# Graph kernel: dealing the steps of the next pair's preparation out between the groups of slots of each gather

## The chip, the cores and the metric

The kernel runs on one core of a Trainium2 chip. The time is device microseconds of one launch. Before the change the median of three runs was 3244.12 us (3240.37 to 3251.95). One further execution was recorded by the hardware profiler; its own time was 3232.01 us. In what follows PE is the tensor engine, DVE the vector engine, ACT the scalar engine, POOL the GpSimd engine, and SP the engine that only issues transfers. Each takes its own queue of instructions.

## The reference

There are 16 graphs of 1024 nodes with 64 channels, each with its own 1024x1024 adjacency matrix. Two layers, each with a residual, are computed:

```
h = relu(layernorm(x))                       # layer 0
neigh = (adj > 0) & not self;  nb = neighbours of a node;  rank = position of a neighbour in its row
skip = ceil(nb / 2) if nb > 10 else 1
drop neighbour j of i if skip > 1 and rank % skip == skip - 1      (and symmetrically j, i)
s = sort of the live neighbours' h, itself included, for each channel
agg = .25 * quantile(s, .25) + .5 * quantile(s, .5) + .25 * quantile(s, .75)   # interpolated
x = x + (relu((h + agg) W1 + b1) W2 + b2)
h = relu(layernorm(x))                       # layer 1
x1, x2, x3 = three steps of bn(relu(adj (x W) + b)), each from the one before
x = x + relu(concat(x1, x2, x3) Wl + bl)
```

The costly part is the sort: for each of 16 x 1024 nodes and 64 channels, some 11 to 42 values are put far enough in order to read three quantiles.

## The kernel before

**Pairs.** Two graphs are handled together, one in each half of the 128 partitions (64 channels each), so there are 8 pairs. Nodes are renumbered by their number of live neighbours, so that columns with like counts stand together. They are cut into seven blocks of columns plus a tail of 16 columns (`BLOCKS`, `TAIL`); a block of 200 columns has 11 slots for neighbours, the last 48 columns have 26, and the tail 42. The tails of four pairs (then of the other four) are sorted together in the fifth and in the last pair (`TAILS`).

**Preparation of a pair.** `prepare` is a generator, which yields after each of 81 small steps. For each of the two graphs `prepare_one` loads the adjacency matrix in eight tiles `a`, converts them (`edge` L662 on ACT, `junk_v` L664 on DVE) and transposes them on PE (`ptE` L669, evicted to `edgeT` L672), counts the neighbours (`tot` L643, `sums` L648, `nbp` L683, `nb` L687), numbers and drops neighbours (`cs` L708 and L713, `stays` L717 and L718, `q` L728 to L739, `edge` L744), makes a key per node (`key` L750, `keys` L755) and from it the node's place in the order (`place` L765 on DVE). POOL then scatters the rows to their places in DRAM with eight indirect transfers (L770). `find_live` loads them back in eight tiles `lp` (L786, from POOL's queue, with two buffers), transposes them on PE (`pt` L796) and counts again (`nv_all` L808); `number_slots` writes to `r` (L838) the number of the slot that a neighbour takes. `half` and `z` (L611, L614) are what the quantiles need; `z` is the first thing that a pair's first gather and sort have, and is taken below as the pair's start.

**Gather and sort of a block.** `gather` goes through a block's slots in groups. For a group, DVE compares `r` with the slot's number and writes a 0/1 matrix `s` (L962, two buffers), PE multiplies the features `hp` with it into `pg` (L993, three PSUM buffers), and ACT copies `pg` to `g` (L998). `sort_block` runs a network of minima and maxima over the slots on DVE (L920), weights them (L925, L933; coefficients on ACT, L855 and L858) and sends the sums to DRAM (`store`, with a transposition `pt_agg` L1005).

**Second half of the net.** `later` is also a generator. For a pair it loads what is needed and gathers agg back into the order of the nodes with 16 indirect transfers on POOL (L1172), adds h (L1071), and runs the small multiplications of layer 0 and the three steps of layer 1 (`pw` L1113, `pg` L1129, `py` L1084).

**Order.** In the main loop, while pair p is gathered and sorted block by block, the preparation of pair p+1 goes on: ahead of the gather of each next block stand 11 steps of it. At the eighth turn the rest is run, and the next pair's first block is gathered. In the last pair there is nothing left to prepare, and 7 steps (`STEPS`) of `later` take their place:

```
for p in range(NP - 1):
    ahead = Steps(prepare(p + 1, early))
    for n in range(last + 1):
        for _ in range(11):
            ahead.step()
```

The order in which the program is written is a priority only. A scheduler, with costs of its own for each instruction, decides from the priorities and the dependencies the order in which each engine's queue holds its instructions; on the chip that order is fixed.

Of the kernel before, what the change touches and what calls it, by code (L numbers as in the profile page):

```python
# [29 lines left out]
STEPS = 7  # L30
# [329 lines left out]
def missing_high(slots, least):  # L360

    return range(slots - 1, least, -2)
# [37 lines left out]
def graph_layers_kernel(ctx: ExitStack, tc: tile.TileContext, ins, out: bass.AP):  # L400
    nc = tc.nc
    x_d, adj_d, mask_d = ins["x"], ins["adj"], ins["nodemask"]
    NB, N, _ = x_d.shape
# [96 lines left out]
    def column(name, rows, twice=False):  # L500
        t = const.tile([rows * (1 + twice), 1], F32, name=f"c_{name}")
        for k in range(1 + twice):
            nc.scalar.dma_start(out=t[k * rows : (k + 1) * rows, :], in_=ins[name].rearrange("(p o) -> p o", o=1))
        return t
# [19 lines left out]
    for i in (1, 2, 3):  # L524
        wl = const.tile([P, P], F32, name=f"wl{i}")
        both(wl, ins[f"L1_gnn_W{i}"])
        bl, g, be, m, v = (column(f"L1_gnn_{k}{i}", C, True) for k in ("b", "g", "be", "m", "v"))
# [16 lines left out]
    def bias(value):  # L544

        if value not in biases:
            t = const.tile([P, 1], F32, name=f"bias{len(biases)}")
            nc.vector.memset(t, value)
            biases[value] = t
        return biases[value]  # L550
# [382 lines left out]
            nc.vector.tensor_tensor(o, a, b, ALU.add)  # L933
            i -= k

    def gather(st, block, g, pools):


        work, ps, _ = pools
        j0, j1, least, slots = block  # L940
        first, end, fewer = NEAR[(BLOCKS + (TAIL,)).index(block)]
        W = j1 - j0
        high = missing_high(slots, least)
        r, at = (st.r[0], j0) if j1 <= SPLIT else (st.r[1], j0 - SPLIT)
        per = max(1, min(HALF // W, 400 // W))
        for k0 in range(0, slots, per):
            n = min(per, slots - k0)

            w0 = fewer.get(k0, 0)
            if w0 == W:  # L950
                w0 = 0
            chunks = [
                range(
                    max([c for c in first if k0 + k >= first[c]], default=0),
                    min([c for c in end if k0 + k < end[c]], default=NT),
                )
                for k in range(n)
            ]
            s = work.tile([P, n, 2, NT, W], BF16, tag="s", bufs=2, name="s")
            for k, us in enumerate(chunks):  # L960
                us = slice(us.start, us.stop)
                nc.vector.tensor_scalar(  # L962
                    s[:, k, :, us, w0:], r[:, :, us, at + w0 : at + W], float(LIVE + 1 + k0 + k), None, ALU.is_equal
                )
            pg = ps.tile([P, n, W], F32, tag="pg", bufs=3, name="pg")
            looks = [(u, [k for k in range(n) if u in chunks[k]]) for u in range(NT)]
            looks = sorted((look for look in looks if look[1]), key=lambda look: -len(look[1]))
            whole = len(looks[0][1]) == n and not w0
            if not whole:
                for x in range(2):  # L970

                    nc.tensor.matmul(
                        out=pg[x * C : (x + 1) * C].rearrange("p k w -> p (k w)"), lhsT=ident_h[C:, :C],
                        rhs=st.hp[C:].rearrange("p a x t c -> p (a x t c)")[:, : n * W], start=True, stop=False,
                    )
            for i, (u, ks) in enumerate(looks):
                if i == whole:
                    for k in range(n):
                        if k0 + k + 1 not in high:
                            continue  # L980
                        none = work.tile([P, W], BF16, tag="none", bufs=2, name="none")
                        nc.scalar.activation(
                            none, st.nvs[:, j0:j1], AF.Relu, bias=bias(k0 + k + 0.5), scale=-1.0
                        )
                        for x in range(2):
                            half = slice(x * C, (x + 1) * C)
                            nc.tensor.matmul(
                                out=pg[half, k], lhsT=ident_big[:, half], rhs=none, start=False, stop=False
                            )
                ks = slice(ks[0], ks[-1] + 1)  # L990
                for part in range(3):
                    for x in range(2):
                        nc.tensor.matmul(  # L993
                            out=pg[x * C : (x + 1) * C, ks, w0:], lhsT=st.hp[:, part, x, u, :],
                            rhs=s[:, ks, x, u, w0:], start=(whole and i == 0 and part == 0),
                            stop=(i == len(looks) - 1 and part == 2),
                        )
            nc.scalar.copy(g[:, k0 : k0 + n, :], pg)  # L998
# [9 lines left out]
        for x in range(2):  # L1008
            nc.scalar.dma_start(out=agg_d[2 * p + x][place0 : place0 + n, :], in_=o[:n, x * C : (x + 1) * C])

    def gather_block(st, n, pools):
        work, ps, rows = pools
        block = (BLOCKS + (TAIL,))[n]
        j0, j1, _, slots = block
        if n == 0:
            for q in range(len(TAUS)):
                nc.gpsimd.tensor_copy(tail_z[:, q, st.p, :], st.z[:, q, TAIL[0] : TAIL[1]])
        st.g[n] = rows.tile([P, slots, j1 - j0], F32, tag="g", bufs=2, name="g")
        gather(st, block, st.g[n], pools)

    def sort_block(st, n, pools):

# [326 lines left out]
    with ExitStack() as stack:  # L1349
        keep = stack.enter_context(tc.tile_pool(name="keep", bufs=1))  # L1350
        pools = (
            stack.enter_context(tc.tile_pool(name="work", bufs=1)),
            stack.enter_context(tc.tile_pool(name="ps", bufs=1, space=PSUM)),
            stack.enter_context(tc.tile_pool(name="rows", bufs=1)),
        )
        last = len(BLOCKS)
        with ExitStack() as inner:
            early = (
                inner.enter_context(tc.tile_pool(name="early", bufs=1)), keep,
                inner.enter_context(tc.tile_pool(name="ps_early", bufs=1, space=PSUM)),  # L1360
            )

            ahead = Steps(prepare(0, early))
            ahead.rest()
            st = ahead.result
            gather_block(st, 0, pools)
            for p in range(NP - 1):
                ahead = Steps(prepare(p + 1, early))
                for n in range(last + 1):
                    for _ in range(11):  # L1370
                        ahead.step()
                    if n == 0 and p in TAILS:

                        sort_block(st, n, pools)
                        gather_block(st, n + 1, pools)
                        sort_tails(*TAILS[p], pools)
                        continue
                    if n < last:
                        gather_block(st, n + 1, pools)
                    else:  # L1380
                        ahead.rest()
                        gather_block(ahead.result, 0, pools)
                    sort_block(st, n, pools)
                st = ahead.result


        with ExitStack() as inner:
            one = inner.enter_context(tc.tile_pool(name="late", bufs=1))
            late = (one, inner.enter_context(tc.tile_pool(name="ps_late", bufs=2, space=PSUM)))
            done = Pair()  # L1390
            done.sent = TAILS[NP - 1][0]
            ahead = Steps(later(late, done))
            for n in range(last + 1):
                for _ in range(STEPS):
                    ahead.step()
                if n == 0:
                    sort_block(st, n, pools)
                    gather_block(st, n + 1, pools)
                    sort_tails(*TAILS[NP - 1], pools)
                    done.sent = NP - 1  # L1400
                    continue
                if n < last:
                    gather_block(st, n + 1, pools)
                sort_block(st, n, pools)
            done.sent = NP
            ahead.rest()
# [46 lines left out]
```

## Time and profile before

| What | Value |
|---|---|
| median of three runs | 3244.12 us |
| profiled execution, its own time | 3232.01 us |
| its span, first to last instruction | 3230.2 us |
| granted clock of the tensor engine | 0.902 |
| DVE, PE, ACT, POOL busy | 2569.1, 2602.9, 1714.2, 461.8 us |
| preparation of the first pair | 0 to 196 us |
| start of the eight pairs (`z`, L614) | 196, 496, 803, 1110, 1421, 1800, 2113, 2418 us |
| last pair with `later` beside it | 2418 to about 2913 us |
| rest of `later` | about 2913 to 3230 us |

A pair thus takes 300 to 314 us, the one in which tails are sorted 379 us. Busy shares are means over stages with different limits, so single stretches are looked at. In a line of the waits, the left side is the instruction that waited, the right side what came last before it could start, and then follow total us, number of times and the longest. In a timeline, the time in brackets is how long the engine had been idle, and what ended that.

### The profile page before, as it was taken

Reading aid. Unit: us, or ns where it says so; the run is one execution under the profiler, and the core shown is the slowest. Engines: PE = TensorE matmul, PEld = TensorE weight load, DVE = VectorE, ACT = ScalarE, POOL = GpSimd, SP = SyncE. Lnnn points to the kernel's source line nnn. Section 1 sums busy time; section 2 is a strip of 40 time slices with the busy share of each in tenths; the row PEclk is TensorE's granted clock in tenths of the full one; section 3 lists DMA queues with packets and bytes.
Section 4 is the critical chain, followed back from the end, with each engine's and each line's share of the span. In section 5 each row is a group of like instructions: output and inputs, shape, how many; then the busy total and the mean of one; then the engine's idle time right before and its main releaser. Section 6 shows DMA issues by size and latency. Waiting matters only on the chain. (4 is left out here: it accounts for less than half of the span.)

```text
span 3230.2 us, 67236 instructions
## 1 busy us (share of the span) xinstructions
PE 2602.9 (81%) x27819; PEld 1728.7 (54%) x27849; DVE 2569.1 (80%) x5895; ACT 1714.2 (53%) x3292; POOL 461.8 (14%) x545
## 2 busy tenths in 40 slices
PE   3689968987898689867686799689976689898878
PEld 2446645664566357545463466456644356565545
DVE  4149999899889988998997889988996888793332
ACT  4777647655766566666464666476553223242221
POOL 4111020110011001200112010201112120221110
PEclk9779989998999799988797799889988799899999
DMA  4131113011311130114001211130102110222211
GB/s 136 46 105 66 37 44 123 33 35 32 118 33 37 42 107 33 51 54 97 31 17 45 91 48 34 45 117 32 39 21 61 21 42 17 54 55 53 53 53 41
DMA packets 221082, 177.45 MB, mean 55 GB/s; under 512 B 189024, under 2 KB 189152, under 8 KB 216672
## 3 DMA queue, kind: packets, MB, share of 16 engines
q1 hardware_dynamic: 141824, 125.88, 12.7%
q0 software_dynamic: 17408, 37.81, 3.8%
q10 hardware_dynamic: 61536, 9.39, 1.9%
q8 instruction: 219, 3.59, 0.5%
q14 instruction: 95, 0.78, 0.1%
HBM read 124.44 MB, written 48.55 MB: 54 GB/s over the span
## 5 line engine op out<-in xcount | busy, mean ns | idle before, releaser
L993 PE MATMUL pg<-s,hp 128*64 128x400 bf16 (+11 forms) x16848 | 1361.8, 314 | 93.2 <-DVE s L962 92.7
L993 PEld LDWEIGHTS <-hp 128*64 128x64 bf16 x16848 | 907.4, 113 | 452.1 <-issue 75.3
L962 DVE TENSOR_SCALAR s<-r 128x3200 bf16<-128x3200 bf16 (+25 forms) x1312 | 621.1, 520 | 144.2 <-PE pg L993 143.9
L998 ACT COPY g<-pg 128x400 f32<-128x400 f32 (+10 forms) x384 | 168.5, 442 | 478.2 <-PE pg L993 440.4
L920 DVE TENSOR_TENSOR t<-g 128x600 f32<-128x600 f32 (+9 forms) x524 | 319.8, 628 | 12.9 <-ACT g L998 11.1
L770 POOL DMA_INDIRECT live_d<-edge,place x128 | 175.4, 1371 | 1025.3 <-DVE place L765 870.9
L1129 PE MATMUL pg<-adjT,xw 128*64 128x512 fp8e4 x2304 | 285.5, 400 | 39.6 <-DVE xw L1119 28.9
L920 DVE TENSOR_TENSOR g<-t 128x96 f32<-128x96 f32 (+16 forms) x555 | 285.8, 539 | 1.4
L855 ACT ACTIVATE coef<-z,bias 128x200 f32<-128x200 f32 (+6 forms) x480 | 174.8, 402 | 140.9 <-DVE agg L933 133.7
L1129 PEld LDWEIGHTS <-xw 128*64 128x64 bf16 x2304 | 144.7, 115 | 163.1 <-DVE xw L1119 30.3
L1172 POOL DMA_INDIRECT agg<-agg_d,place x128 | 139.4, 1089 | 535.7 <-PE pt L1060 412.8
L920 DVE TENSOR_TENSOR t<-t 128x192 f32<-128x192 f32 (+20 forms) x447 | 208.5, 478 | 0.4
L796 PE MATMUL pt<-ident_h,lp 128*128 128x128 bf16 x1024 | 102.3, 261 | 120.8 <-DMA lp<-live_d 71.1
L786 POOL DMA_DIRECT2D lp<-live_d x128 | 87.5, 685 | 774.0 <-PE pt L796 745.4
L664 DVE SCALAR_TENSOR_TENSOR junk_v<-a 128x1024 fp8e4<-128x1024 f32 x128 | 156.3, 1221 | 49.2 <-DMA a<-in_adj 49.0
L858 ACT ACTIVATE coef<-coef,wcol 128x200 f32<-128x200 f32 (+7 forms) x512 | 190.7, 399 | 3.5 <-issue 2.2
L799 ACT ACTIVATE liveT<-pt 128x1024 fp8e4<-128x1024 f32 x128 | 129.9, 1024 | 98.7 <-PE pt L796 97.6
L838 ACT CAST r<-pr 128x592 bf16<-128x592 f32 (+1 forms) x256 | 143.5, 587 | 48.6 <-PE pr L834 47.4
L832 PE MATMUL pr<-liveT,upto 128*128 128x512 fp8e4 (+2 forms) x384 | 124.7, 343 | 50.3 <-ACT r L838 41.3
L796 PEld LDWEIGHTS <-lp 128*128 128x128 fp8e4 x1024 | 82.9, 117 | 145.0 <-DMA lp<-live_d 101.0
L762 ACT ACTIVATE junk<-keys,minus 128x1024 fp8e4<-128x1024 f32 x128 | 144.4, 1128 | 29.8 <-PE keys L755 28.7
L744 ACT ACTIVATE edge<-q,bias 128x1024 fp8e4<-128x1024 f32 x128 | 142.0, 1110 | 33.1 <-PE q L739 29.1
(182 smaller groups left out, 3956.6 us busy)
## 6 DMA issues: line engine op xcount, KB each, us to landing
a<-in_adj SPq DMA_DIRECT2D x128, 512.0 KB, 3.4
adjT_d<-edgeT SPq DMA_DIRECT2D x16, 1024.0 KB, 4.4
lp<-live_d POOLq DMA_DIRECT2D x128, 128.0 KB, 2.3
adjT<-adjT_d SPq DMA_DIRECT2D x16, 1024.0 KB, 6.3
room<-in_x SPq DMA_DIRECT2D x16, 256.0 KB, 3.2
h_d<-room SPq DMA_DIRECT2D x16, 256.0 KB, 2.9
h_again<-h_d SPq DMA_DIRECT2D x16, 256.0 KB, 3.8
xt<-in_x SPq DMA_DIRECT2D x16, 256.0 KB, 4.7
```

What stands on the lines that cost most here:

```text
L664: nc.vector.scalar_tensor_tensor(junk, a, 1.0, a, ALU.is_equal, ALU.not_equal, accum_out=odd[:, b, t : t + 1], saturate=False)
L762: nc.scalar.activation(junk, keys, AF.Sign, bias=minus[:, t : t + 1], accum_out=above[:, t : t + 1], saturate=False)
L770: sent = nc.gpsimd.indirect_dma_start(out=live_d[b][:, :], out_offset=bass.IndirectOffsetOnAxis(ap=place[:, b, t : t + 1], axis=0), in_=ed ...
L796: nc.tensor.matmul(out=pt[:, u, :], lhsT=lp[:, u * P : (u + 1) * P], rhs=ident_h, start=True, stop=True)
L838: nc.scalar.copy(st.r[side][:, x, u, :], pr[:, : j1 - j0])
L855: nc.scalar.activation(coef[:, i, :], z[:, at], AF.Abs, bias=bias(rank - (slots + 1) // 2 + tau), scale=sign)
L858: nc.scalar.activation(coef[:, i, :], coef[:, i, :], AF.Relu, bias=wcol[:, q : q + 1], scale=-w)
L920: nc.vector.tensor_tensor(view(bufs, o, n1, n2), view(bufs, a, n1, n2), view(bufs, b, n1, n2), ALU.max if op else ALU.min)
L962: nc.vector.tensor_scalar(s[:, k, :, us, w0:], r[:, :, us, at + w0 : at + W], float(LIVE + 1 + k0 + k), None, ALU.is_equal)
L993: nc.tensor.matmul(out=pg[x * C : (x + 1) * C, ks, w0:], lhsT=st.hp[:, part, x, u, :], rhs=s[:, ks, x, u, w0:], start=(whole and i == 0 an ...
L998: nc.scalar.copy(g[:, k0 : k0 + n, :], pg)
L1129: nc.tensor.matmul(out=pg[cs, :], lhsT=part[:, u, cs], rhs=adjT[x][:, u, sl], start=(u == 0 and k == 0), stop=(u == NT - 1 and k == len(xw ...
```

## The change

`gather` takes a generator of steps and a number, and runs that many steps spread evenly over the groups of slots: ahead of each group as many as are due by the slots that are then done. The 11 (in the last pair 7) steps ahead of each gather fall away. So a gather whose block has, say, five groups has one to three steps ahead of each group. The number of steps for each block is the same, and the steps themselves are the same; ahead of the next pair's first gather the rest of the preparation is still run whole, now without the 11 steps before it (four steps are then left, the same as before). In the two turns with tails, and in the first turn of the last pair, the sort of the first block now stands ahead of the steps. In the last turn of the last pair the 7 steps stay as they were.

```diff
-    def gather(st, block, g, pools):
+    def gather(st, block, g, pools, between):
...
         for k0 in range(0, slots, per):
             n = min(per, slots - k0)
+            if between is not None:
+                steps, count = between
+                for _ in range(count * (k0 + n) // slots - count * k0 // slots):
+                    steps.step()
...
-        gather(st, block, st.g[n], pools)
+        gather(st, block, st.g[n], pools, between)
...
             for p in range(NP - 1):
                 ahead = Steps(prepare(p + 1, early))
                 for n in range(last + 1):
-                    for _ in range(11):
-                        ahead.step()
                     if n == 0 and p in TAILS:
 
                         sort_block(st, n, pools)
-                        gather_block(st, n + 1, pools)
+                        gather_block(st, n + 1, pools, (ahead, 11))
                         sort_tails(*TAILS[p], pools)
                         continue
                     if n < last:
-                        gather_block(st, n + 1, pools)
+                        gather_block(st, n + 1, pools, (ahead, 11))
                     else:
                         ahead.rest()
                         gather_block(ahead.result, 0, pools)
...
             for n in range(last + 1):
-                for _ in range(STEPS):
-                    ahead.step()
                 if n == 0:
                     sort_block(st, n, pools)
-                    gather_block(st, n + 1, pools)
+                    gather_block(st, n + 1, pools, (ahead, STEPS))
                     sort_tails(*TAILS[NP - 1], pools)
                     done.sent = NP - 1
                     continue
                 if n < last:
-                    gather_block(st, n + 1, pools)
+                    gather_block(st, n + 1, pools, (ahead, STEPS))
+                else:
+                    for _ in range(STEPS):
+                        ahead.step()
                 sort_block(st, n, pools)
```

More of the change, by code (lines that the diff above doesn't have):

```diff
@@ L1009, in store, with gather_block @@
             nc.scalar.dma_start(out=agg_d[2 * p + x][place0 : place0 + n, :], in_=o[:n, x * C : (x + 1) * C])
-    def gather_block(st, n, pools):
+    def gather_block(st, n, pools, between=None):
         work, ps, rows = pools
```

## The prediction

> **What bounds the kernel now.** I read the busy times first, then the stretches, then the waits of one stretch, then single events.
>
> ```profile
> PE 2602.9 (81%) x27819; PEld 1728.7 (54%) x27849; DVE 2569.1 (80%) x5895; ACT 1714.2 (53%) x3292; POOL 461.8 (14%) x545
> ```
>
> Two engines are equally full, so the bound changes by place. The stretch from 520 to 840 us, a pair and the start of the next, has PE busy 271.3 and DVE 292.2 of 320 us: inside the pairs DVE leads. From 2900 us on DVE is busy 117.1 of 330 and PE 269.8: the tail after the last sort is PE's. The chain of the page covers 3% of the span, so I did not use it. Waits of DVE and PE in 520 to 840 us (engine, waiting line, what came last: total us, times, longest):
>
> ```profile
> DVE s L962 <- PE pg L993: 14.5, 10, 3.0
> DVE junk_v L664 <- DMA a<-in_adj: 6.6, 8, 1.9
> ...
> PE pt_agg L1005 <- DVE agg L933: 13.2, 4, 10.3
> PE pt L796 <- DMA lp<-live_d: 7.5, 3, 5.4
> ...
> PE pg L993 <- DVE s L962: 6.2, 4, 3.9
> PE q L728 <- ACT edge L744: 2.4, 1, 2.4
> ```
>
> DVE loses some 27 us per pair, half of it because the two buffers of `s` are still being read by matmuls. Only work that closes these holes can make a pair shorter; its 292 us of DVE work stay.
>
> The last view is the timeline of the fourth period (z of L614 at 803 us): start, duration, operation, and idle time before it. On POOL, scatters and loads of live rows share one queue:
>
> ```profile
> 1014.92 1.10 POOL L770 DMA_INDIRECT live_d<-edge,place  x1 [7.48 <-DVE place L765]
> ...
> 1025.54 2.40 POOL L770 DMA_INDIRECT live_d<-edge,place  x1 [0.31 <-ACT liveT L799]
> 1027.94 1.40 POOL L786 DMA_DIRECT2D lp<-live_d  x2
> ```
>
> On PE and on DVE, what came after:
>
> ```profile
> 1030.41 0.40 PE L796 MATMUL pt<-ident_h,lp 128*128 128x128 bf16 x2 [5.48 <-DMA lp<-live_d]
> ...
> 1038.97 1.86 DVE L962 TENSOR_SCALAR s<-r 128x1152 bf16<-128x1152 bf16 x5 [2.74 <-PE pg L993]
> ```
>
> The reader should see one chain. The second graph's place (L765, 211.7 us into the pair) releases eight scatters, 13 us of POOL. Behind them stand the sixth to eighth load of the first graph. PE waits 5.5 us for the sixth, gather groups queue behind that, and DVE waits 2.7 us for their buffer.
>
> **What the Trainium skill says.** "Perfetto Trace Analysis", section "Tensor Engine Instruction", calls ACT, DVE and GPSIMD strict FIFO and gives PE only a limited reorder. The lines above agree: nothing passes the blocked tile. "DMA: Bandwidth & Descriptors", section "Anatomy of one DMA", puts about 2 us of fixed cost on a GpSimd DMA; loads of live rows here land in 2.3 us. "SBUF — State Buffer", section "A bandwidth-pool intuition that's wrong", says that some VectorE operations lock GpSimd out of writing descriptors. The trace may show it once: most scatters take 1.0 to 1.5 us, but in the pair with tails, at 1689.0 us, one took 14.4 us.
>
> **The change part by part.** I compared the order of each engine's instructions in the two built programs and gave every instruction its duration of before. Positions below are so much work into a pair's queue. No instruction is added in the seven pairs, POOL's order is unchanged, and SP's loads of `a` move by a place or two against the adjT_d store. PE's and DVE's sequences are the same at the start of a pair (to 39 and 54 us of work) and at its end (DVE from 286 us on). So only holes between can change.
>
> *First graph.* Groups 9 and 12 of `s` come earlier on DVE (58.1 to 54.1, 83.6 to 73.3); key and place of the first graph later (111.9 to 132.2, 126.9 to 137.8). Before, PE waited 3.9 us for `s` at 47.7 us into the pair, 2.3 for agg at 90.3, and smaller pieces for edgeT and nbp; behind these it ran 12.3 us behind its own work through the second gather. In the new order I find a lag of 9.6. DVE follows PE there: its waits from 124.6 to 136.1 us are 0.7, 1.9, 2.5 and 2.8, together 7.9. It gains the 2.7 and some of the next groups' slack, taken as 3.5. Against it, nb (L687) of the second graph now reaches DVE ahead of its sums and nbp on PE: about 1.8. Net -1.7, at most -6 if all of the 7.9 falls but that 1.8. PE's 2.4 us wait for edge (L744) also goes, but PE then waits for lp anyway: nothing.
>
> *Second graph.* Its place moves on DVE from 216.1 to 231.5 us of work; on the old clock that is from 211.7 to 225.1 us, +13.4. Each step keeps its own price: 0.5 to the first scatter, 13 for eight, 2.5 for the load, hence 241.1 us. PE comes to the sixth tile 4.9 us of work later (208.8 to 213.7) with a lag larger by 1.1: at 227.9 instead of 221.9. It stands for 13.2 us, where it stood 5.5. The group cut in two by this tile feeds `s` of group 41, which stands 3.7 us earlier on DVE (249.3 to 245.6). DVE has some 4.6 us to spare, so it waits 8.6 instead of 2.7: +5.9, and about +1 for the next groups, which follow PE. Tiles 13 to 16 are now spread among gather groups (+3.4 to +7.9), so the 2.4 us wait at 273.4 us goes: -2.4. Later slips of PE fall into its 10.3 us wait for agg at 292.8, the cover at the end: were it gone, they would cost up to 5. Net +4.5.
>
> A pair: -1.7 + 4.5 = +2.8; I take +2, because part of the +1 behind the tile may find slack too. Bounds are -4 (all first-graph holes close, the tile costs only +2) and +9 (nothing gained, lateness reaches DVE whole). Seven pairs: +14. In the pair with tails the 21.3 us that DVE lost at 307.9 us belong to the long scatter. I take it as recurring; without it that pair is 17 us shorter.
>
> *Last stage.* Its sums (L1071) wait for indirect gathers:
>
> ```profile
> DVE agg L1071 <- DMA agg<-agg_d,place: 50.1, 5, 15.2
> DVE s L962 <- PE pg L993: 18.4, 8, 4.5
> ```
>
> Sixteen gathers take POOL some 20 us and 2.4 to land. The DVE work between the first issue and L1071 is, before to after, 10.6 to 61.7 us for the second pair (its wait was 15.2: gone), 20.4 to 21.9 for the third (10.4, -1.3), 17.9 to 16.3 for the fourth (11.9, +1.4), and 42.5 to 30.3 for the fifth (1.6, +10.6 if the queue is as late). Sum -4.5. PE has 8.5 us less done when the tails are sorted, part of which returns in the PE-bound rest, estimated at 1.5. Net -3, bounds -15 and +12. The some 318 us after 2913 us are the same instructions: 0.
>
> *Sum.* The profiled execution took 3232.0 us (span 3230.2). 3232.0 + 14 - 3 = 3243. The median shown is 3244.12, 12.1 above it; with that, 3255.
>
> **The rivals.**
>
> *Clearly slower.* A longer lateness per pair. For it: the scatter that took 14.4 us shows that this queue can lose more than its 13 us, and place now falls among the dense small operations of the fifth and sixth sort. Against: the other pairs' scatters show no such loss. With +9 a pair: 3232 + 63 - 3 + 12 = 3304.
>
> *Faster.* The other side, by one mechanism: DVE's waits on `pg` in the first half are holes that the old clumps of preparation make on PE. Dealt out, PE keeps ahead. With -4 in seven pairs: 3232 - 28 - 3 + 12 = 3213. It decides where PE's stand at the sixth tile stays under some 10 us: DVE then waits under 5.8, which with +1 and -2.4 costs less than the 1.7 gained. For it: the 14.5 us of waits. Against: the position of place, which is a fact of the queue.
>
> *No change.* The program's order is only a priority, both ends of a pair are in the same order, and gains and losses cancel: 3244. For it: only 25 us of holes exist in a normal pair. That the deal hardly alters the queues is excluded by the positions above.
>
> **How the numbers follow.** A difference of 0.3%, about 10 us, is what a measurement of this kernel can tell from none. Forecast 0.38, own range 3246 to 3275; its low end, 0.05, counts as the same. Clearly slower 0.22, no change 0.18, faster 0.22. So faster 0.22, same 0.05 + 0.18 = 0.23, slower 0.33 + 0.22 = 0.55. The range leaves out a tenth on each side: 3222 to 3305, between the rivals' ends.
>
> **What would show it.** Right: in a normal pair the DVE wait for `pg` near 235 us into it grows from 2.7 to about 8 us, PE's wait for lp from 5.5 to about 13, place of the second graph falls some 10 us later, and the group of waits at 124 to 136 us shrinks by 3 us. In the last stage the 15.2 us wait at L1071 is gone and the fifth grows. Pair periods of 300 to 311 us become some 2 us longer. Wrong: if periods fall, the lp wait was absorbed; if they rise by 8 or more, look at the scatters' durations and at what POOL waits for. It would also fail if the tails or the L1071 waits change by more than 15 us.

## The result

| | before | after |
|---|---|---|
| median | 3244.4 us (4 runs, 3240.4 to 3252.0) | 3289.6 us (4 runs, 3280.5 to 3293.5) |
| profiled execution, span | 3230.2 us | 3278.5 us |
| ratio | | 1.0133 (95% interval 1.0110 to 1.0157) |

The change costs some 45 us. The time lies inside the predicted range (3222 to 3305), on the predicted side, but above the forecast's own range (3246 to 3275) and four times as far from no change as the forecast had it, nearer to the rival that was called clearly slower (3304). Both profiled executions had a mean granted clock of 0.902.

The busy times of the page of the changed kernel:

```profile
PE 2620.0 (80%) x27826; PEld 1725.6 (53%) x27849; DVE 2568.8 (78%) x5895; ACT 1709.4 (52%) x3292; POOL 474.0 (14%) x545
```

DVE has the work it had (2569.1 us before), and its share fell: the 48 us by which the span grew are holes, stretches in which DVE waits. Where they are, the distances between the pairs' starts (L614) tell:

| stage | before, us | after, us | difference |
|---|---|---|---|
| six pairs without tails, sum | 1842.5 | 1897.5 | +55.0 (+14.2 in the first pair, +3.8 in the sixth) |
| pair with tails | 379.2 | 372.3 | -6.9 |
| last stage, to the last sum of the sort | 495.1 | 490.6 | -4.5 |
| preparation of the first pair, and the rest of `later` after the sort | | | +4.6 |

A pair without tails loses 9.2 us on average. Lines of the `gather` stand four lower in the changed kernel (L962 is L966, L993 is L997, L998 is L1002). Take the period that the prediction reads (called the fourth there, the first being the preparation ahead of the first pair): before it ran from 802.7 to 1110.2 us, now from 828.5 to 1146.5. Waits of DVE:

```profile
DVE s L966 <- PE pg L997: 24.4, 6, 11.3
DVE t L920 <- ACT g L1002: 3.5, 2, 2.8
...
DVE key L750 <- ACT edge L744: 3.0, 1, 3.0
```

and of PE:

```profile
PE pt L796 <- DMA lp<-live_d: 11.7, 2, 9.8
PE pt_agg L1009 <- DVE agg L933: 9.4, 3, 8.1
...
PE pg L997 <- DVE s L966: 5.9, 2, 4.3
PE keys L755 <- DVE key L750: 5.2, 2, 2.8
```

In the same period before, `s` waited in ten shorter pieces, DVE had no wait for key, and PE's wait for it was 0.5 us:

```profile
DVE s L962 <- PE pg L993: 16.0, 10, 2.8
```

Now there are fewer waits and longer ones. They are in two places.

**The second graph.** The timeline of POOL (start, duration, operation, idle time before):

```profile
1055.80 4.32 POOL L770 DMA_INDIRECT live_d<-edge,place  x1 [2.51 <-DVE s L966]
...
1069.47 0.96 POOL L770 DMA_INDIRECT live_d<-edge,place  x1 [0.30 <-issue]
1070.43 1.15 POOL L786 DMA_DIRECT2D lp<-live_d  x2
```

then that of PE and of DVE:

```profile
1072.90 1.89 PE L796 MATMUL pt<-ident_h,lp 128*128 128x128 bf16 x16 [9.79 <-DMA lp<-live_d]
...
1079.59 1.56 DVE L966 TENSOR_SCALAR s<-r 128x864 bf16<-128x864 bf16 x5 [11.32 <-PE pg L997]
```

It is the chain that the prediction described. The second graph's place comes 226.8 us into the pair (before 211.7), its scatters hold POOL until 241.9 (before 225.2), the loads of the first graph's live rows stand behind them, PE waits 9.8 us for one, and DVE 11.3 us for the group behind it. Waits of DVE in this pair from 142 us on sum to 16.0 us, against some 8 before.

**The first graph.** DVE in the gather of the third block, from 126 to 142 us into the pair, at each line the idle time before it:

```profile
954.98 0.17 DVE L750 SCALAR_TENSOR_TENSOR key<-nv,node 128x8 f32<-128x8 f32 x1 [3.04 <-ACT edge L744]
...
963.74 1.33 DVE L966 TENSOR_SCALAR s<-r 128x2112 bf16<-128x2112 bf16 x2 [7.85 <-PE pg L997]
965.79 1.51 DVE L966 TENSOR_SCALAR s<-r 128x2464 bf16<-128x2464 bf16 x2 [0.73 <-PE pg L997]
970.06 1.62 DVE L920 TENSOR_TENSOR t<-g 128x1400 f32<-128x1400 f32 x1 [2.75 <-ACT g L1002]
```

These are 14.4 us. The prediction had expected the waits of this place (7.9 us) to shrink; counting from 45 to 142 us, DVE waits some 4 us more than before. The last line is the first operation of the next sort, and waits for the last copy of its gather. ACT's queue at that moment:

```profile
968.57 1.15 ACT L762 ACTIVATE junk<-keys,minus 128x1024 fp8e4<-128x1024 f32 x1
969.57 0.24 ACT L762 ACTIVATION_READ_ACCUMULATOR junk<-keys,minus 128x1 f32 x1
969.66 0.37 ACT L1002 COPY g<-pg 128x200 f32<-128x200 f32 x1
```

Seven of the eight activations that rank the first graph's keys, and two evictions of edgeT, now lie ahead of the last copy of this gather. Before, the last of the eight was over well ahead of that copy:

```profile
923.22 1.11 ACT L762 ACTIVATE junk<-keys,minus 128x1024 fp8e4<-128x1024 f32 x1
...
940.32 0.33 ACT L998 COPY g<-pg 128x200 f32<-128x200 f32 x1 [1.02 <-PE pg L993]
```

Place of the first graph was at 121.9 us into the pair, and is now at 143.1.

This period is not quite the average. Over the six pairs without tails, DVE's waits in the first 142 us of a pair grew by 15.4 us in all, and those after it by 40.4: some 2.6 us of a pair's loss belong to the first part, and 6.7 to the second.

### The profile page after: what moved, and what is told of

It reads as the page before. It is cut to its first block, busy times and chain, and to the rows that moved or that the text cites. A ratio compares the mean times of both kernels' runs of the same rounds, so it can differ in the third digit from the quotient of the medians.

```text
span 3278.5 us, 67218 instructions
## 1 busy us (share of the span) xinstructions
PE 2620.0 (80%) x27826; PEld 1725.6 (53%) x27849; DVE 2568.8 (78%) x5895; ACT 1709.4 (52%) x3292; POOL 474.0 (14%) x545
## 5 line engine op out<-in xcount | busy, mean ns | idle before, releaser
L997 PE MATMUL pg<-s,hp 128*64 128x400 bf16 (+11 forms) x16848 | 1406.4, 318 | 130.5 <-DVE s L966 123.0
L997 PEld LDWEIGHTS <-hp 128*64 128x64 bf16 x16848 | 913.8, 114 | 512.6 <-issue 102.2
L966 DVE TENSOR_SCALAR s<-r 128x3200 bf16<-128x3200 bf16 (+25 forms) x1312 | 622.3, 522 | 168.9 <-PE pg L997 163.3
L1002 ACT COPY g<-pg 128x400 f32<-128x400 f32 (+10 forms) x384 | 168.5, 442 | 399.8 <-PE pg L997 383.8
L1176 POOL DMA_INDIRECT agg<-agg_d,place x128 | 156.7, 1225 | 517.3 <-PE pt L1064 190.0
L786 POOL DMA_DIRECT2D lp<-live_d x128 | 79.4, 622 | 765.3 <-PE pt L796 677.8
L662 ACT ACTIVATE edge<-a 128x1024 fp8e4<-128x1024 f32 x128 | 134.1, 1054 | 89.2 <-DMA a<-in_adj 88.4
L832 PE MATMUL pr<-liveT,upto 128*128 128x512 fp8e4 (+2 forms) x384 | 121.9, 334 | 64.1 <-ACT r L838 54.9
L717 ACT ACTIVATE stays<-cs,back 128x1024 f16<-128x1024 f32 x128 | 137.1, 1115 | 58.9 <-DVE look L698 41.4
```

Source lines behind the costliest of these rows:

```text
L966: nc.vector.tensor_scalar(s[:, k, :, us, w0:], r[:, :, us, at + w0 : at + W], float(LIVE + 1 + k0 + k), None, ALU.is_equal)
L997: nc.tensor.matmul(out=pg[x * C : (x + 1) * C, ks, w0:], lhsT=st.hp[:, part, x, u, :], rhs=s[:, ks, x, u, w0:], start=(whole and i == 0 an ...
L1176: nc.gpsimd.indirect_dma_start(out=agg[:, t, x, :], out_offset=None, in_=agg_d[b][:, :], in_offset=bass.IndirectOffsetOnAxis(ap=place[:, b ...
```

## The experiments

The theory after this reading: **A**, the loss of the second graph is POOL's queue; **A'**, the loss of the first graph comes from key and ranking, which stand too near the end of their gather. Rival **B**: dealing out as such disturbs, each gather its share. All ratios are to runs of the kernel before on the same chip, whose median there was 3225.6 to 3239.5 us, so ratios are compared, not times. A point is a hundredth of the ratio; a difference between two such ratios is known to some 0.3 or 0.4 points.

### One gather undone, then the other, then both (e1, e2, e3)

```diff
-                    if n < last:
+                    if n in (3,):            # e2: (1,)   e3: (1, 3)
+                        for _ in range(11):
+                            ahead.step()
+                        gather_block(st, n + 1, pools)
+                    elif n < last:
                         gather_block(st, n + 1, pools, (ahead, 11))
```

> The deal is undone for one gather only: the eleven steps with key and place of the second graph (ahead of the gather of the fifth block) stand ahead of it again, in all seven pairs; all else is dealt out. Theory A (the scatters of the late place of the second graph stand in POOL's queue before the loads of live rows, and PE, then DVE wait for these: some 8 us of each pair's 10): place returns to about 212 us into the pair, the 11 us wait of DVE for pg behind the tile goes, the median falls from 3289.6 by 45 to 56 us, to 3234 to 3245. Theory of the prediction (4.5 of second graph against a gain of the first): a fall of about 32, to 3258. Rival B (the deal as such disturbs, each gather its share): a fall of a seventh, some 7 us, to 3283.

Measured: 3234.3 us, ratio 0.998 (0.9964 to 0.9997). Of the seven gathers dealt out, this one holds as much as the whole loss, or more: 1.5 points of 1.33. Place is back at 213.6 us into the fourth period, and of the 11.3 us wait 4.4 are left; the first graph's waits (3.0, 4.9, 0.7, 3.8) stay. No wait of `s` is over 4.9 now:

```profile
DVE s L966 <- PE pg L997: 13.9, 6, 4.9
```

> The deal is undone for one gather only, the one with key and place of the first graph (the gather of the third block). Theory A' (the first graph's eight junk activations, which rank the keys, now stand in ACT's queue ahead of the last copies of that gather, and DVE waits for those: some 4 us of a pair's 10): the waits for key, s and t from 126 to 142 us into the pair return to those of before, and the median falls by 20 to 30 us, to 3260 to 3270. Theory of the prediction (dealing the first graph gains 1.7 us per pair): it rises by about 12, to 3301. Rival B: falls by 7, to 3283.

Measured: 3259.7 us, ratio 1.0072 (1.0044 to 1.0100), 0.6 points or some 20 us better than the change. The prediction's own account of this part, that dealing it gains, would have given a worse time. The wait of key is gone, the 11.2 us wait of the second graph stays.

> Both gathers of e1 and e2 undone; those of the second, fourth, sixth, seventh and eighth block, and the last stage, stay dealt out. Theory A with A': the sum of both, a fall of 65 to 80 us, to 3210 to 3225, which would be faster than before; if the two losses share one wait, some 50, to 3240. Rival B: a fall of 14, to 3276.

Measured: 3217.6 us, ratio 0.994 (0.991 to 0.997). The gains are 1.5, 0.6 and, together, 1.9 points: nearly a sum, so they are two losses. B is refuted: two gathers of seven carry all of it, and with the other five dealt out the kernel is faster than before. That is not the merit of the deal in general: in the profile 17 us are gained in the pair with tails (362.0 against 379.1), where a scatter of 14.4 us is absent (see the last section), the six other pairs take 1836.6 us against 1842.5, and the last stage is 13 longer.

### Taking the loads out of POOL's queue (e4, e5, e6)

```diff
-                load = nc.gpsimd.dma_start(out=lp, in_=live_d[b][t * P : (t + 1) * P, :])
+                load = nc.sync.dma_start(out=lp, in_=live_d[b][t * P : (t + 1) * P, :])      # e4
+                queue = nc.sync if x == 0 and t >= 2 else nc.gpsimd                          # e5, e6
+                load = queue.dma_start(out=lp, in_=live_d[b][t * P : (t + 1) * P, :])
```

> The changed kernel, with the loads of live rows (L786) issued from SP's queue and not from POOL's, so that they no longer stand behind the second graph's scatters; place stays as late as in the changed kernel. Theory A: PE's wait for the sixth tile (9.8 us) falls under 3 and DVE's 11 us wait under 3, the median falls by 45 to 60, to 3230 to 3245. If the loss is not in POOL's queue but in the order on PE (tiles, nv_all and gather groups mixed): stays above 3275. If SP's loads are slower to land than POOL's 2.3 us (loads of a land in 3.4), up to 15 us of the gain are lost.

Measured: 3307.8 us, ratio 1.0207 (1.0179 to 1.0235), worse than the change. By the number alone it is the case over 3275, in which the loss would lie in the order on PE; that it would be worse than the change was not expected at all. The waits of DVE in the fourth period tell why:

```profile
DVE s L966 <- PE pg L997: 16.4, 8, 7.8
DVE edgeT L678 <- DMA adjT_d<-edgeT: 7.4, 1, 7.4
```

The wait behind the late tile fell from 11.3 to 2.1 us, but on SP the first two loads stand ahead of the store of adjT_d, wait for the scatters of the first graph, and hold that store up; edgeT's next writer waits 7.4 us for it. A queue was cleared and another one blocked, so the time of this run tells A neither right nor wrong. The last stage, in which nothing was changed, was 18 us longer in this profile than in that of the changed kernel (see the last stage below), so this wait is not all of the ratio.

> e4 moved all loads of live rows and made the store of adjT_d wait behind two of them on SP (a new wait of 7.4 us at edgeT, L678, in each pair). Here only the six loads that can stand behind the second graph's scatters move to SP (first graph, third to eighth tile), in the changed kernel; place of the second graph stays late. Theory A: the 11 us wait of DVE falls under 3, no new wait at L678, a fall of 45 to 60 us against the changed kernel's 3289.6, to 3230 to 3245. If the loss lies in the order on PE and not in POOL's queue: above 3275.

Measured: 3218.0 us, ratio 0.9968 (0.9955 to 0.9982), 1.65 points better than the change. In the fourth period DVE's waits are (lines of the gather and the sort stand one lower than in the changed kernel):

```profile
DVE s L967 <- PE pg L998: 12.2, 5, 4.9
DVE t L921 <- ACT g L1003: 4.5, 2, 3.8
DVE junk_v L664 <- DMA a<-in_adj: 3.5, 6, 1.0
DVE key L750 <- ACT edge L744: 3.0, 1, 3.0
```

The 11.3 us are gone (the longest wait is now one of the first graph's), no wait at L678 has come, and the first graph's waits stay. Place stays late, at 225.6 us, and no other step of the program is moved: it is the queue. The six pairs without tails take 1841.9 us, as before the change.

> The same move of six loads in the kernel before, as a control. Theory A: it takes away PE's wait of 5.5 us and DVE's of 2.7 us per pair, and the 21 us of the pair with tails where that comes: a fall of 10 to 40 us against the kernel before. If moving the loads helps by something other than the queue, the fall is as large as in e5.

Measured: 3204.9 us, ratio 0.9924 (0.9895 to 0.9952): 0.76 points in the kernel before, half of what it gives after. So of the change's 1.33 points, 0.89 (1.65 less 0.76) are this queue, and 0.44, some 14 us, remain with the queue cleared in both. What e6 gains does not lie where it was expected in every pair, though: in its profile it lies in the pair with tails (358.2 us against 379.1), where DVE no longer waits behind the long scatter, and not in the six other pairs (1843.7 against 1842.5). e5 gains all the 55 us of those. Where the 0.44 points lie was not settled.

### The ranking of the first graph (e7, e8, e12)

```diff
+            w = N // 4 if x == 0 else N
             nc.scalar.activation(
-                junk, keys, AF.Sign, bias=minus[:, t : t + 1], accum_out=above[:, t : t + 1], saturate=False
+                junk[:, :w], keys[:, :w], AF.Sign, bias=minus[:, t : t + 1], accum_out=above[:, t : t + 1],
+                saturate=False
             )
-        nc.vector.tensor_scalar(place[:, b, :], above, -0.5, 0.5 * (N - 1), ALU.mult, ALU.add)
+        if x == 0:
+            nc.vector.scalar_tensor_tensor(place[:, b, :], above, 0.0, node, ALU.mult, ALU.add)
...
```

This kernel leaves out three quarters of the first graph's ranking and takes the node numbers as its places.

> The changed kernel, with the first graph's eight ranking activations (junk, L762) cut to a quarter of the columns, which leaves out three quarters of that graph's ranking (its places are then the node numbers, and the flag for counts outside the blocks is zeroed); some 4 to 5 us less of ACT per pair, in the same places of the queues. Theory A' (DVE waits for copies of g that stand behind these activations in ACT's queue): the waits of s and t at 132 to 142 us into a pair fall by 3 to 4 us, the median by 20 to 28, to 3262 to 3270. If these waits come from key and PE (L750, L755) and not from ACT's queue: a fall under 7.

Measured: 3254.0 us, ratio 1.0076 (1.0047 to 1.0104), 0.57 points or 18 us better than the change, a little less than expected. In the same place as above, DVE now reads (lines five lower):

```profile
953.71 0.71 DVE L971 TENSOR_SCALAR s<-r 128x2112 bf16<-128x2112 bf16 x1 [4.91 <-PE pg L1002]
...
957.12 1.51 DVE L971 TENSOR_SCALAR s<-r 128x2464 bf16<-128x2464 bf16 x2 [1.18 <-PE pg L1002]
958.54 1.61 DVE L925 TENSOR_TENSOR t<-g 128x1400 f32<-128x1400 f32 x1
```

The sort no longer waits for this copy in any of the six pairs without tails; in the changed kernel it waits 2.8 to 3.8 us for it in each. The long wait of `s`, here 4.9 and not 7.9, is another matter: with the whole ranking it is 4.9 in e1 and e5 as well. It goes with PE's time for the keys, in the changed kernel and in e7:

```profile
955.20 3.78 PE L755 MATMUL keys<-ident,key 128*128 128x128 f32 x16 [2.80 <-DVE key L750]
```

```profile
948.11 2.05 PE L755 MATMUL keys<-ident,key 128*128 128x128 f32 x16 [2.81 <-DVE key L750]
```

The granted clock in these moments was 0.50 and 1.00. In other pairs of e7, where the keys took 3.4 to 3.8 us, `s` waits 6.3 to 7.8 us.

> The same shorter ranking of the first graph in the kernel before, as a control. Theory A': there the activations end some 15 us before the last copies of that gather, so the fall is under 7 us. If shorter ACT work helps everywhere: 20 or more.

Measured: 3220.8 us, ratio 0.9974 (0.9964 to 0.9984), some 8 us, slightly over what was allowed. So 10 us of e7's 18 would be owed to where the ranking stands after the change; the intervals can't tell these 10 from none, and in the profiles 5.6 us (e8) and 7.2 us (e7) are gained in the preparation of the first pair. What shows A' for the wait of the copy is that wait itself, which is gone. The 4.9 us of `s` and the 3.0 us of key are not ACT's ranking, since they stay: key waits for the last edge, PE waits 2.8 us for key (keys, L755), and gather groups stand behind that.

In e12 the whole deal stays, but the eleven steps of this gather come at twice the pace, so within its first half:

```diff
+                pace = 2 * count if block is BLOCKS[2] and count == 11 else count
-                for _ in range(count * (k0 + n) // slots - count * k0 // slots):
+                for _ in range(min(count, pace * (k0 + n) // slots) - min(count, pace * k0 // slots)):
                     steps.step()
```

> The changed kernel, with the eleven steps of the third block's gather dealt at twice the pace, so within its first half: key of the first graph stands at 120.6 us of DVE work (before 111.9, changed kernel 132.2, e2 111.9), the second graph as in the changed kernel. If the first graph's loss comes from how near the end of its gather key and the ranking stand: most of e2's gain of 0.6% comes back, ratio 1.006 to 1.009, and the wait of t for g at 140 us goes. If it comes from dealing the steps among the groups at all: stays at 1.012 or above.

Measured: 3241.4 us, ratio 1.0050 (1.0036 to 1.0064), slightly better than was expected, and no worse than e2 with no deal there at all. In the same period the waits of key and of `t` at this place are gone (a wait of 2.0 us for place has come), and the second graph's wait stays at 11.0. It is the nearness to the gather's end, not the dealing.

### The last stage, and a faster kernel (e9, e10, e11)

e9 deals out the last stage alone. e10 is e3 with the last stage of before. e11 is e10 with the six loads of e5.

> Only the last stage is dealt out; the seven pairs are as before. The prediction took -3 for it (-15 to +12); the profile of the changed kernel has that stage at 490.6 us against 495.1, those of e1, e3 and e4, with the same order of work there, at 506.7 to 508.5. If the first of these is typical: the ratio to before is 0.997 to 1.000. If the others are: 1.002 to 1.005.

Measured: 3232.4 us, ratio 1.0017 (1.0006 to 1.0028): a cost of some 5 us where the prediction had a gain of 3. The profiled execution, with 3223.0 us one of the fastest, doesn't show where they are lost. The waits at the sum of layer 0, in the last stage of before, of the change and of e1, which has the same steps there as the change:

| | waits at the sum, us | last stage, us |
|---|---|---|
| before | 50.1 | 495.1 |
| change | 40.4 | 490.6 |
| e1 | 55.3 | 506.7 |
| e9 | 43.6 | 491.9 |
| e10 (order of before) | 45.9 | 489.0 |

The 15.2 us wait of the second pair's sum fell as predicted, to nothing in the change and e9, to 8.2 in e1; but the fourth grew from 11.9 to some 17.6, and the fifth from 1.6 to between 6.5 and 9.1. In the four profiles with the order of before in which it was read, apart from the first, the stage took 489.0 to 492.7 us; in those with the deal 490.6 to 508.5. Why the longer of these (506.7 to 508.5, in e1, e3 and e4) have a longer second and third wait was not settled.

> e3 with the last stage as before: dealt out are only the gathers of the second, fourth, sixth, seventh and eighth block of the seven pairs. If dealing the last stage costs some 10 us: ratio 0.989 to 0.992, a version faster than e3 (0.994) and than before. If it costs nothing: 0.993 to 0.995.

Measured: 3187.7 us, ratio 0.989 (0.9859 to 0.992). The step from e3 to e10 is larger than e9 accounts for: in the profiles the pairs without tails are some 3 us shorter too, so it is not all the last stage's. Against the kernel before, these six pairs take 1819.0 us and not 1842.5, the pair with tails 358.6 and not 379.1.

> e10 with the six loads of live rows issued from SP, as in e6. The best of both, if they are independent: e6 has 0.9924 and e10 some 0.991, together 0.983 to 0.987. If what e3 and e10 gain is the same POOL queue that e6 clears (the pair with tails: 362 us against 379): no better than 0.990.

Measured: 3176.7 us, ratio 0.9842 (0.9816 to 0.9867). It lies where it was expected (0.983 to 0.987), and beats both kernels, by 1.6% and by 2.9%. The pairs without tails take 300.5 to 304.8 us, and the one with tails 355.1.

## Why the prediction was right and where it was wrong

**Direction and range: right,** and the mechanism of the larger loss was named with its place. The size was not: the forecast was 3255, with 3275 as its own upper end, and 3289.6 was measured. That it fell inside the whole range is owed to the room that the range left for the slower rival, not to the sum.

**Second graph: right in kind, short by half.** Place at 225.1 on the old clock: measured 226.8. The tile's rows at 241.1: they came at 244.4, POOL being done with the scatters at 241.9. DVE's wait of 8.6: measured 11.3. The stand of PE of 13.2 was 9.8, since PE itself came some 7 us later, held among others by a wait of 2.4 us for the second graph's key. Three terms were off: eight scatters took 14.6 us and not 13 (the first alone 4.3); the 2.4 us wait at 273 us did not go (2.5 at 282); and PE's lateness did not fall into the cover at the end as taken, the 10.3 us wait for agg, which shrank only to 8.1. Net +8 in this period, +6.7 on average, instead of +4.5.

**First graph: wrong, and this is the step that failed.** "It gains the 2.7 and some of the next groups' slack, taken as 3.5": DVE lost 3.6 us in this period, 2.6 on average, where the net of this part was put at -1.7. PE did get to work earlier there (groups 16 to 18 of the period were copied 15 to 19 us sooner), and this is the gain that the prediction saw. But "key and place of the first graph later" was written down for DVE and then not costed. It moved a serial chain, edge to key to keys to ranking, to the end of a gather whose result the next sort needs at once, and put seven activations of 1.1 us ahead of the last copy in ACT's queue. The prediction speaks of the order on PE, DVE, POOL and SP, and says nothing of ACT's. It had itself quoted "Perfetto Trace Analysis" of the Trainium skill, section "Tensor Engine Instruction", that ACT is strict FIFO as well, and here the copy that ended at 970.0 us stood behind the ranking.

**A pair: +2 forecast, +9.2 measured,** just past the +9 that was given as its bound and as the clearly slower rival's price. That the rival's price fits is in part luck: it named the lateness of the scatters alone, and the first graph's share was in neither.

**Pair with tails.** The long scatter was taken as recurring; the trace of the change has none over 4.3 us, and the pair became 6.9 us shorter. The step had its size: 17 us for the absence, against which stand the 11.1 us that DVE now waits there as in other pairs.

**Last stage.** Forecast -3, bounds -15 and +12: +5 by e9. Which waits go and which grow was right, apart from their sizes: their sum is -9.7 in the profile of the change, the shortest of that order, against -4.5 forecast, and +5.2 in e1.

**"No change"** did not come; the positions had moved. The **faster** rival's condition, PE's stand under 10 us, was met at 9.8, yet DVE's wait was 11.3: it took 4.6 us of slack off PE's stand, and PE's own later arrival, by some 7 us, had used that up.

## What to carry to other kernels

When work is dealt out evenly over a stage, walk each chain that ends in it on every queue, the scalar engine's too: a serial step moved from a stage's start to its end is paid by whatever the next stage needs first, and here the holes filled elsewhere didn't repay that. A queue that carries both the sends of one job and the loads of another turns lateness of the first into a wait of the second. Moving six loads to another queue was worth 1.65 points after the change and 0.76 before it; moving all sixteen of a pair cost 0.74, and there a store stood behind two of them. In this kernel the best was to deal out only the five other gathers of a pair (e10), and to move the six loads as well (e11).

## What was not expected of the hardware

One scatter of the pair with tails takes 14.40 us in each profile with the order of before, here in the kernel before and in e9 (one line each: shortest, median and longest in ns; first and last start), and none does in the changed kernel:

```profile
L770 POOL DMA_INDIRECT live_d<-edge,place x128: 957/1144/14401, 108.4 to 2336.8; - x128
```

```profile
L770 POOL DMA_INDIRECT live_d<-edge,place x128: 956/1138/14398, 108.1 to 2332.4; - x128
```

```profile
L770 POOL DMA_INDIRECT live_d<-edge,place x128: 959/1214/4322, 109.4 to 2394.1; - x128
```

It is thus no accident of a run, but goes with the order of the instructions around it. The lock that "SBUF — State Buffer" of the Trainium skill describes (section "A bandwidth-pool intuition that's wrong") lasts until the VectorE operation ends. The longest operation of DVE that began in these 14.4 us took 1.6 us, so one alone doesn't explain it; DVE was busy without a gap, and whether a row of operations could, no run here shows.

The keys of the first graph took PE 2.05 us at a granted clock of 1.00 in each of the six pairs without tails in every profile where key stands away from the end of its gather (before, e2, e3, e6, e8, e12). Where it stands at the end (the changed kernel, e1, e4, e5, e7), they took 2.7 to 3.8 us at 0.50 to 0.73 in 16 of 30 such pairs, and `s` then waits up to 7.9 us and not 4.9. PE had stood still for 2.8 us ahead of both of the lines shown with e7, of which one has the low clock and one the full. What lowers the clock there was not tested.
